# Second-pass products in 64-column tiles, matrix loads in four transfers, and four changed planner settings, in a four-layer graph network on one core

## The chip, the cores and the metric

The kernel runs on one core of a Trainium2 chip. The metric is the device time of one execution in microseconds (us), and lower is better. Before the change it is 1319.26 us, the median of three runs (1314.0 to 1320.12).

## What is computed

There are 32 graphs with 512 nodes and 128 features each (`x`), and one 512 x 512 matrix `adj` of zeros and ones for each graph. Four layers follow one another. Each takes `h = relu(layernorm(x))` and adds its result to `x`:

```python
# 0: masked attention
q, k, v = relu(h @ Wq.T + bq), relu(h @ Wk.T + bk), relu(h @ Wv.T + bv)
x = x + softmax(clip(q @ k.T * adj, 0, 9e13) - 9e15 * (1 - adj)) @ v
# 1: graph convolution, gated by an LSTM that runs over the last 128 nodes' convolved rows
x = x + sigmoid((A_norm @ h) @ lstm(conv(h[:, -128:, :])))
# 2: four sub-layers, each with adj and its transpose, row and column norms, and a tanh
# 3: adj @ (h @ W.T) + bias, with a leaky slope for negative values
```

The LSTM has 128 steps, and each step needs the state `h` of the step before. A step treats all 32 graphs together. It reads only the last 128 nodes of each graph, so attention for those nodes must be finished for every graph before the first step.

## The kernel before

The work is done in three stages. `pass_1` (one call per graph) computes keys, values and the attention of the last 128 nodes, stores keys and values in DRAM, and prepares the LSTM's input. `pass_2` (one call per graph) computes the attention of the other 384 nodes. `rest` does layers 1 to 3 for one graph. The LSTM (`lstm`) runs beside `pass_2`: while one step's cell waits for ScalarE and VectorE, TensorE works on second-pass products.

The second pass of a graph loads keys (`keys`), the normalised input (`hT`), the adjacency matrix (`a`), the values (`v`) and `x`. Line 1303 makes the queries `f_pq`, line 1312 four score blocks `f_s` of 128 x 384, line 1315 their exponentials `f_e`, line 1316 multiplies them by the mask, and line 1321 sums twelve products with the values into `f_po`. Line 1327 adds the result to `xc`, which line 1332 stores in DRAM as `dx`.

All these products are float32. One is issued as two matmul instructions, each with its own weight load. The helper `quarters` (line 1274) cuts a product into four tiles of 32 columns (`TURN`), each a quarter of the output's partitions: eight matmuls and eight weight loads for a product of 128 columns. The LSTM's products `f_z` (line 1223) are also tiles of 32 columns, because their weights are the state of 32 graphs. A step has 16 matmuls: eight with the state of the step before, and eight that prepare a later step's input.

For the graphs in `EARLY` (0 to 23) the second pass goes on. It squares the matrix into `ar` on ScalarE with a row sum (`squares`, line 1360, four operations of one row block each), normalises `xc` in place (lines 1054 and 1057), and makes the first graph sum `f_pg` (line 1406, eight matmuls of 128 x 512 on the whole array), which is stored and read back in `rest`. For the two graphs in `FIRST` (26 and 27) only the squares are made early. For the others the second pass loads 384 columns of the matrix, and `rest` loads it again, whole, in one transfer, and makes the squares and the first sum there. The second pass of the last four graphs (`LATE`) is planned beside `rest`.

The order of the instructions on each engine is fixed when the kernel is built, by a planner (`Plan`). Every operation has a rank, a duration that was written in by hand, and for transfers a `gap`, the time until the data is taken to have landed. The planner lets time run and gives each free engine the lowest-ranked operation that can start. LSTM operations have the lowest ranks. `foresee` notes when the LSTM will next want an engine, and another operation isn't started if it would hold that engine longer than `patience` beyond this time:

```python
elif held is not None and s < held < s + o.engines[e][0] - o.patience:
    continue
```

`patience` is 0.15 us, for the sums of line 1406 `PATIENCE`, 1.3 us. A `SWITCH` time (0.2 us into 128-column products, 0.1 us into tiled ones) is counted where a tiled product meets an untiled one. All tiled products count as one kind. `LANDED` (3.8 us) is the gap of the second pass's loads; other transfers take 2.0. Transfers are issued by SP in the planned order, in one queue.

Operations name the tiles that they read and write, whole (`a`) or by part (`(a, t)`); a whole one conflicts with every part. In the kernel before, line 1291 writes the whole of `a`, and each square reads the whole of it.

Of the kernel before, what the change touches and what calls it, by code (L numbers as in the profile page):

```python
# [13 lines left out]
P = 128  # L14
# [744 lines left out]
def symmetric(ctx, tc, x, adj, weights, cols, rows, lstm_b, prelu_a, out, fail):  # L759
# [12 lines left out]
    nc = tc.nc  # L772
    B, N, D = x.shape
    NT = N // P
    T = P
    L = NT - 1
    NR = N - P
    MANY = 512 // (4 * B)
    LATE = 4
    FIRST = [B - LATE - 2 + k for k in range(2)]  # L780
    EARLY = range(24)
    FOLDS = (4, 7, 10, 13)
    MOVED = range(2, B - 2)
    TURN = 32
    T_STEP = 0.22
    SOON = 9_950.0
    LANDED = 3.8
    PATIENCE = 1.3
    plan_rest = 30_000
    assert D == P and N == 512  # L790

# [14 lines left out]
    def flat(ap):  # L806
        return ap.rearrange("p a b -> p (a b)")

    def f32(ap):
        return ap.bitcast(FP)  # L810
# [5 lines left out]
    def new(tag, shape, name, dtype=FP):  # L816
        return plan.cell(sb, tag, shape, dtype, name)
# [8 lines left out]
    def t_r(n):  # L826
        return max(0.112, n * 0.000455)
# [9 lines left out]
    def t_dma(kb):  # L837
        return 0.1 + kb / 315.0

    def PE(rank, t, fn, r=(), w=(), **k):  # L840
        return plan.op({"PE": (t, fn)}, rank, r, w, **k)

    def ACT(rank, t, fn, r=(), w=(), **k):
        return plan.op({"ACT": (t, fn)}, rank, r, w, **k)
# [7 lines left out]
    def DMA(rank, kb, fn, r=(), w=(), **k):  # L852
        return plan.op({"SP": (max(0.45, t_dma(kb)), fn)}, rank, r, w, gap=k.pop("gap", 2.0), **k)
# [178 lines left out]
    def ln_stats(rank, xc, tiles, name, at=0):  # L1032

        st = new("st", (P, NT, 6), f"f_st_{name}")
        mv = new("mv", (P, NT, 2), f"f_mv_{name}")
        for t in tiles:
            DVE(rank, 0.19, lambda t=t: nc.vector.bn_stats(st.t[:, t, :], xc.t[:, t - at, :]), [(xc, t - at)], [(st, t)])
        for t in tiles:
            DVE(rank, 0.09, lambda t=t: nc.vector.bn_aggr(mv.t[:, t, :], st.t[:, t, :]), [(st, t)], [(mv, t)])
        return mv  # L1040
# [8 lines left out]
    def ln_apply(rank, xc, mean, rstd, shift, r, name, relu=False, place=None):  # L1049

        xn = place or new("xn", (P, NT, P), f"f_xn_{name}")
        for t in range(NT):
            def dve(t=t):
                nc.vector.tensor_scalar(xn.t[:, t, :], xc.t[:, t, :], mean(t), rstd(t), OP.subtract, OP.mult)

            def act(t=t):
                nc.scalar.activation(xn.t[:, t, :], xc.t[:, t, :], AF.Relu, bias=shift(t), scale=rstd(t))
            either = {"ACT": (t_act(P) + 0.13, act)}
            if not relu:
                either["DVE"] = (t_dve(P), dve)  # L1060
            plan.op(either, rank, [(xc, t)] + r, [(xn, t)])
        return xn
# [209 lines left out]


    def quarters(product):
        for k in range(P // TURN):
            product(slice(k * TURN, (k + 1) * TURN))

    def pass_2(b):
        R = 20_000 + b * 10 if b < B - LATE else 30_000 + (b - B + LATE) * 10 + 15
        dkq, dv, dl, dx = kept[b]  # L1280
        early = b in EARLY
        whole = early or b in FIRST
        a = new("a" if whole else "ar", (P, NT, N if whole else NR), f"f_a_{b}")
# [3 lines left out]
        xc = new("x", (P, NT if whole else L, P), f"f_x2_{b}")  # L1287
        DMA(R, 192, lambda: nc.sync.dma_start(hT.t, dkq.t[:, N:]), [dkq], [hT], gap=LANDED)
        DMA(R, 256, lambda: nc.sync.dma_start(keys.t, dkq.t[:, :N]), [dkq], [keys], gap=LANDED)
        if whole:  # L1290
            DMA(R, 1024, lambda: nc.sync.dma_start(a.t, adj[b].rearrange("(t p) j -> p t j", p=P)), [], [a], gap=LANDED)
            ar, deg = squares(R, b, a, "2")
            mask, rows_of = ar, lambda j: f32(ar.t[:, j, :NR])
        else:
            DMA(R, 768, lambda: nc.sync.dma_start(a.t, adj[b, :, :NR].rearrange("(t p) j -> p t j", p=P)), [], [a], gap=LANDED)
            mask, rows_of = a, lambda j: a.t[:, j, :]
        DMA(R, 258, lambda: nc.sync.dma_start(v.t, dv.t), [dv], [v], gap=LANDED)
        DMA(R, 192, lambda: nc.sync.dma_start(xc.t[:, :L, :], x[b, :NR].rearrange("(t p) d -> p t d", p=P)), [],
# [30 lines left out]
        if whole and not early:  # L1329
            begun[b] = a, xc, ar, deg  # L1330
        else:
            DMA(R + 5, 192, lambda: nc.sync.dma_start(dx.t, xc.t[:, :L, :]), [(xc, t) for t in range(L)], [dx])
        mv = ln_stats(R, xc, range(L), f"r{b}")
        l1 = lns[b]
        POOL(R, 0.15, lambda: nc.gpsimd.tensor_copy(ln1[:, b, 0, :L], mv.t[:, :L, 0]), [mv], [(l1, "mr")])
# [19 lines left out]
    def squares(rank, b, a, name):  # L1355

        ar = new("ar", (P, NT, N), f"f_ar{name}_{b}", FR)
        deg = new("dg", (P, NT), f"f_deg{name}_{b}")
        for t in range(NT):
            ACT(rank, 0.62, lambda t=t: nc.scalar.activation(ar.t[:, t, :], a.t[:, t, :], AF.Square,  # L1360
                                                             accum_out=deg.t[:, t : t + 1]), [a], [(ar, t), (deg, t)])
        return ar, deg

    def diagonal(rank, ar, op):
# [5 lines left out]
    def sums_of_1(rank, b, xc, ar, rs):  # L1370
# [4 lines left out]
        xs = ln_apply(rank, xc, lambda t: ln1[:, b, 0, t : t + 1], lambda t: rs.t[:, t : t + 1], lambda t: sh.t[:, t : t + 1],  # L1375
                      [l1, rs, sh], f"c{b}", place=xc if b in EARLY else None)
        xp = relu_parts(rank, xs, f"c{b}")
        pg = bank(f"f_pg_{b}")
        diagonal(rank, ar, OP.add)
        first = aggregate(rank, xp, ar, pg)  # L1380
        gT = xc if b in EARLY else new("gs", (P, N), f"f_gT_{b}")
        evict(rank, N, lambda: gT.t if b not in EARLY else flat(gT.t), lambda: pg.t, [pg], [gT])
        return gT, first
# [10 lines left out]
    def relu_parts(rank, xs, name):  # L1394

        parts = new("y", (P, NT, 2, P), f"f_xp_{name}", FR)
        ACT(rank, 0.52, lambda: nc.scalar.activation(parts.t[:, :, 0, :], xs.t, AF.Relu), [xs], [(parts, 0)])
        DVE(rank, t_dve(N), lambda: nc.vector.scalar_tensor_tensor(  # L1398
            parts.t[:, :, 1, :], xs.t, 0.0, f32(parts.t[:, :, 0, :]), OP.max, OP.subtract), [xs, (parts, 0)], [(parts, 1)])
        return parts  # L1400

    def aggregate(rank, parts, ar, pg):

        def half(k):
            for j in range(NT):
                nc.tensor.matmul(pg.t, parts.t[:, j, k, :], ar.t[:, j, :], start=(k == 0 and j == 0),  # L1406
                                 stop=(k == 1 and j == NT - 1))

        def both():
            half(0)  # L1410
            half(1)
        if rank < plan_rest:
            last = PE(rank, 8 * t_r(N), both, [parts, ar], [pg])
            last.patience = PATIENCE
            return last
        for k in range(2):
            last = PE(rank, 4 * t_r(N), lambda k=k: half(k), [(parts, k), ar], [pg])
        return last

    def rest(b, turn, lw_after):  # L1420
# [12 lines left out]
        l1 = lns[b]  # L1433
        rs = None if b in EARLY else new("rs", (P, NT), f"f_rs_c{b}")

# [12 lines left out]

        if b in EARLY:
            gT, first = new("gs", (P, N), f"f_gT3_{b}"), None  # L1450
# [157 lines left out]
    for b in range(B):  # L1608
        pass_2(b)
        if b in FOLDS:  # L1610
            fold(FOLDS.index(b), 20_000 + b * 10)
# [89 lines left out]
```

## Time and profile before

| | before |
|---|---|
| median of the runs shown | 1319.26 us |
| the profiled execution, its own time | 1317.18 us |
| span of its instructions | 1315.4 us |
| TensorE, weight loads (busy in the span) | 1275.1 us (97%), 974.1 us (74%) |
| VectorE, ScalarE, GpSimd | 992.6 (75%), 833.2 (63%), 392.4 (30%) |
| `f_z` line 1223, 2040 matmuls | 87.0 us |
| `f_s` line 1312, 1024 matmuls | 106.6 us |
| `f_po` line 1321, 3072 matmuls | 108.6 us |
| `f_pq` line 1303, 256 matmuls | 27.7 us |
| instruction fetches | 97 packets, 1.59 MB |
| mean granted clock of TensorE | 0.994 |

Busy time is the time in which at least one instruction of the group has a record open. A record of a matmul lasts longer than its data streams, since its end is modelled, so the pace of the array is read from the distance between the starts of records. A line of the timeline has the start, the time to the end of the merged records, the engine, the line of the code, the operation, what it writes and reads, the shape and the count; in brackets stands idle time before it and what ended it. "issue" means that the engine waited for nothing that the profile shows. A line of waits has the waiting engine and line, what it waited for, the total in us, the number of times and the longest. A line by stretch has the start and end of the stretch, its length, busy time and instruction count of TensorE, its weight loads, VectorE, ScalarE and GpSimd, then TensorE's granted clock, the share of the DMA engines and their GB/s.

### The profile page before, as it was taken

Reading aid. Unit: us, or ns where it says so; the run is one execution under the profiler, and the core shown is the slowest. Engines: PE = TensorE matmul, PEld = TensorE weight load, DVE = VectorE, ACT = ScalarE, POOL = GpSimd, SP = SyncE. Lnnn points to the kernel's source line nnn. Section 1 sums busy time; section 2 is a strip of 40 time slices with the busy share of each in tenths; the row PEclk is TensorE's granted clock in tenths of the full one; section 3 lists DMA queues with packets and bytes.
Section 4 is the critical chain, followed back from the end, with each engine's and each line's share of the span. In section 5 each row is a group of like instructions: output and inputs, shape, how many; then the busy total and the mean of one; then the engine's idle time right before and its main releaser. Section 6 shows DMA issues by size and latency. Waiting matters only on the chain.

```text
span 1315.4 us, 32850 instructions
## 1 busy us (share of the span) xinstructions
PE 1275.1 (97%) x12097; PEld 974.1 (74%) x12098; DVE 992.6 (75%) x3286; ACT 833.2 (63%) x2095; POOL 392.4 (30%) x737
## 2 busy tenths in 40 slices
PE   8999999999899899999999999999999999999997
PEld 6888866666576666777777878778787787787774
DVE  7998877767788786977676767777676777787654
ACT  5666757667587565577566666666666675676423
POOL 4655532212242222443031322313222132242101
PEclk9999999999999899999999999999999999999999
DMA  8888888766777555999576677777777755673311
GB/s 264 257 277 279 274 272 254 250 214 205 225 243 243 151 165 163 216 213 207 130 158 159 155 156 163 164 158 152 154 164 161 165 120 90 151 170 72 49 33 35
DMA packets 300585, 234.50 MB, mean 178 GB/s; under 512 B 138240, under 2 KB 244480, under 8 KB 300416
## 3 DMA queue, kind: packets, MB, share of 16 engines
q1 hardware_dynamic: 283520, 215.54, 59.4%
q0 software_dynamic: 16896, 16.78, 8.1%
q8 instruction: 97, 1.59, 0.5%
q14 instruction: 72, 0.59, 0.1%
HBM read 138.16 MB, written 62.65 MB: 153 GB/s over the span
## 4 chain that ended last, share of the span: by engine, by line
PE 84%; DVE 6%; DMA 4%; ACT 3%; issue 2%; POOL 1%; SPq 0%; ACTq 0%; DVEq 0%; POOLq 0%
PE f_pa L1406 17%; PE f_py L1510 15%; PE f_pa L1521 14%; PE f_pg L1406 9%; PE f_s L1312 4%; PE f_z L1223 4%; PE f_po L1321 4%; PE f_p L1562 2%; PE f_pol L1173 2%; PE f_pk L1130 2%; PE f_pv L1146 2%; PE f_pl L1464 2%; PE f_sl L1163 2%; DMA f_a<-in_adj_dram 2%; PE f_pd L1198 1%
## 5 line engine op out<-in xcount | busy, mean ns | idle before, releaser
L1406 PE MATMUL f_pa<-f_ar,f_y 128*128 128x512 f32 x1024 | 300.5, 430 | 1.6 <-ACT f_y L1389 1.4
L1406 PEld LDWEIGHTS f_pa<-f_ar,f_y 128*128 128x128 f32 x1024 | 189.4, 188 | 77.9 <-issue 39.9
L1510 PE MATMUL f_py<-f_wf,f_n 128*128 128x128 f32 x1280 | 173.8, 275 | 0.0
L1510 PEld LDWEIGHTS f_py<-f_wf,f_n 128*128 128x128 f32 x1280 | 165.0, 191 | 9.6 <-issue 2.4
L1521 PE MATMUL f_pa<-f_n,f_wf 128*128 128x512 f32 x320 | 153.1, 592 | 0.0
L1525 ACT ACTIVATE f_n<-f_pa,f_bcol 128x512 f32<-128x512 f32 x128 | 88.2, 689 | 92.1 <-PE f_pa L1521 92.1
L1360 ACT ACTIVATE f_ar<-f_a 128x512 fp32r<-128x512 f32 x224 | 138.7, 622 | 6.0 <-DMA f_a<-in_adj_dram 4.6
L1389 ACT CAST f_y<-f_py 128x512 fp32r<-128x512 f32 x128 | 74.8, 585 | 102.3 <-PE f_py L1510 95.3
L1478 POOL DMA_DIRECT2D f_das<-f_ar x32 | 27.0, 842 | 370.5 <-ACT f_ar L1360 309.3
L1312 PE MATMUL f_s<-f_q,f_k 128*32 128x384 f32 x1024 | 106.6, 500 | 6.4 <-issue 5.7
L1321 PE MATMUL f_po<-f_v,f_e 128*32 128x129 f32 x3072 | 108.6, 273 | 4.3 <-issue 4.2
L1321 PEld LDWEIGHTS f_po<-f_v,f_e 128*32 128x32 f32 x3072 | 90.7, 110 | 22.8 <-issue 14.2
L1517 DVE TENSOR_TENSOR f_pa<-f_pa,f_inv 128x512 f32<-128x512 f32 x128 | 86.7, 693 | 26.3 <-PE f_pa L1406 25.8
L1390 DVE TENSOR_TENSOR f_y<-f_py,f_y 128x512 fp32r<-128x512 f32 x128 | 87.4, 684 | 22.2 <-ACT f_y L1389 22.2
L1223 PE MATMUL f_z<-f_w,f_seq 128*32 128x128 f32 x2040 | 87.0, 280 | 13.0 <-DVE f_seq L1268 5.9
L1223 PEld LDWEIGHTS f_z<-f_w,f_seq 128*32 128x32 f32 x2040 | 55.1, 110 | 51.0 <-ACT f_e L1315 12.2
L1521 PEld LDWEIGHTS f_pa<-f_n,f_wf 128*128 128x128 f32 x320 | 57.5, 190 | 44.8 <-issue 36.8
L1483 DVE SCALAR_TENSOR_TENSOR f_junk<-f_a,f_aT 128x1024 bf16<-128x1024 f32 x64 | 78.1, 1221 | 3.0 <-DMA f_aT<-f_das 1.1
L1315 ACT ACTIVATE f_e<-f_s 128x384 f32<-128x384 f32 x128 | 61.5, 484 | 26.0 <-PE f_s L1312 14.1
L1406 PE MATMUL f_pg<-f_ar,f_xp_d 128*128 128x512 f32 x256 | 74.2, 413 | 0.3 <-DVE f_xp_d L1398 0.2
L1085 DVE COPY f_hl_d<-f_n 128x1024 uint16<-128x1024 uint16 x28 | 19.4, 693 | 70.9 <-ACT f_n L1525 70.8
L1510 PE MATMUL f_py<-f_wf,f_T_c 128*128 128x128 f32 x448 | 72.8, 275 | 0.0
(203 smaller groups left out, 2763.8 us busy)
## 6 DMA issues: line engine op xcount, KB each, us to landing
f_a<-in_adj_dram SPq DMA_DIRECT2D x56, 1024.0 KB
f_das<-f_ar POOLq DMA_DIRECT2D x32, 512.0 KB, 4.7
f_dkq<-f_kh SPq DMA_DIRECT2D x32, 448.0 KB
f_dv<-f_v SPq DMA_DIRECT2D x32, 258.0 KB
f_v<-f_dv SPq DMA_DIRECT2D x32, 258.0 KB
f_x<-in_x_dram SPq DMA_DIRECT2D x32, 256.0 KB
f_al<-in_adj_dram SPq DMA_DIRECT2D x32, 256.0 KB
f_k<-f_dkq SPq DMA_DIRECT2D x32, 256.0 KB
```

What stands on the lines that cost most here:

```text
L1223: nc.tensor.matmul(z.t[part, k, :, :], h, w[:, m : m + 4, part], start=False, stop=True, skip_group_check=True)
L1312: PE(R, t_mm(NR), lambda s=s, j=j: quarters(lambda p: nc.tensor.matmul(s.t[p], keys.t[:, j * P + p.start : j * P + p.stop], q.t, start=Tru ...
L1321: PE(R, t_mm(P), lambda t=t, j=j: quarters(lambda p: nc.tensor.matmul(po.t[p, t, :], es[j].t[:, t * P + p.start : t * P + p.stop], v.t[:, ...
L1360: ACT(rank, 0.62, lambda t=t: nc.scalar.activation(ar.t[:, t, :], a.t[:, t, :], AF.Square, accum_out=deg.t[:, t : t + 1]), [a], [(ar, t), ...
L1389: ACT(rank, t_act(N), lambda: nc.scalar.copy(parts.t[:, :, 0, :], src.t), [src], [(parts, 0)])
L1390: DVE(rank, t_dve(N), lambda: nc.vector.tensor_sub(parts.t[:, :, 1, :], src.t, f32(parts.t[:, :, 0, :])), [src, (parts, 0)], [(parts, 1)])
L1406: nc.tensor.matmul(pg.t, parts.t[:, j, k, :], ar.t[:, j, :], start=(k == 0 and j == 0), stop=(k == 1 and j == NT - 1))
L1483: nc.vector.scalar_tensor_tensor(junk, flat(a.t[:, 2 * k : 2 * k + 2, :]), 1.0, flat(aT.t[:, 2 * k : 2 * k + 2, :]), OP.mult, OP.not_equal ...
L1510: nc.tensor.matmul(py.t[:, j, :], nodes[n].t[:, bass.ts(j, P)], wf[:, W_F[i] + c, 0, :], start=False, stop=(c == nch - 1), skip_group_chec ...
L1517: before = DVE(R, t_dve(N), lambda pa=pa: nc.vector.tensor_mul(pa.t, pa.t, inv_row.t), [inv_row], [pa])
L1521: nc.tensor.matmul(pa.t, wf[:, W_F[i] + c, 1, :], nodes[n].t, start=False, stop=(c == nch - 1), skip_group_check=True)
L1525: ACT(R, 0.57, lambda pa=pa, n=n, i=i: nc.scalar.activation(n.t, pa.t, AF.Tanh, bias=bcol[:, i : i + 1]), [pa], [n])
```

## The change

`quarters` now makes two tiles of 64 columns instead of four of 32. It is used for the products of lines 1303, 1312 and 1321. The LSTM's tiles stay at 32 columns, and the planner's durations and its one kind of tiled product stay as they are.

The second pass loads the matrix in four transfers, one for each row block, and a square depends on its own row block. In `rest` the load stays one transfer.

Four settings change: `EARLY` is 0 to 21 (graphs 22 and 23 join those whose squares and first sum are made in `rest`), `PATIENCE` is 0.9 us, and a new `STORED`, 5.0 us, is the gap of the store of `xc` on line 1332, in place of the ordinary 2.0 us. The planner works out a new order from all of this.

```diff
-    EARLY = range(24)
+    EARLY = range(22)
 ...
-    PATIENCE = 1.3
+    STORED = 5.0
+    PATIENCE = 0.9
 ...
     def quarters(product):
-        for k in range(P // TURN):
-            product(slice(k * TURN, (k + 1) * TURN))
+        for k in range(0, P, 2 * TURN):
+            product(slice(k, k + 2 * TURN))
 ...
         if whole:
-            DMA(R, 1024, lambda: nc.sync.dma_start(a.t, adj[b].rearrange("(t p) j -> p t j", p=P)), [], [a], gap=LANDED)
+            for t in range(NT):
+                DMA(R, 256, lambda t=t: nc.sync.dma_start(a.t[:, t, :], adj[b, t * P : (t + 1) * P, :]), [], [(a, t)], gap=LANDED)
 ...
         else:
-            DMA(R, 768, lambda: nc.sync.dma_start(a.t, adj[b, :, :NR].rearrange("(t p) j -> p t j", p=P)), [], [a], gap=LANDED)
+            for t in range(NT):
+                DMA(R, 192, lambda t=t: nc.sync.dma_start(a.t[:, t, :], adj[b, t * P : (t + 1) * P, :NR]), [], [(a, t)], gap=LANDED)
 ...
-            DMA(R + 5, 192, lambda: nc.sync.dma_start(dx.t, xc.t[:, :L, :]), [(xc, t) for t in range(L)], [dx])
+            DMA(R + 5, 192, lambda: nc.sync.dma_start(dx.t, xc.t[:, :L, :]), [(xc, t) for t in range(L)], [dx], gap=STORED)
 ...
             ACT(rank, 0.62, lambda t=t: nc.scalar.activation(ar.t[:, t, :], a.t[:, t, :], AF.Square,
-                                                             accum_out=deg.t[:, t : t + 1]), [a], [(ar, t), (deg, t)])
+                                                             accum_out=deg.t[:, t : t + 1]), [(a, t)], [(ar, t), (deg, t)])
```

## The prediction

> **What bounds the kernel now.** I read the page first (TensorE busy 97% of the span, and 84% of the chain that ended last), then busy time by stretch, because the change touches one stage only. The stretch from 184 to 522 us holds the LSTM's products `f_z`; 545 to 1250 is the third stage.
>
> ```profile
> 184.00:522.00 338.00, 313.82 (x6188) 214.42 (x6188) 263.87 (x1083) 229.87 (x814) 87.30 (x163) 0.98 0.67 211
> 545.00:1250.00 705.00, 703.46 (x3809) 550.16 (x3808) 518.51 (x1355) 459.38 (x990) 197.43 (x308) 1.00 0.68 150
> ```
>
> The first pair of numbers after the length is TensorE. In the third stage it is never free, and the change leaves most of its products as they are. In the LSTM stretch 24 us are free, and more is lost that counts as busy, because a matmul's record lasts longer than the array streams. So I took start-to-start times of matmul records: 338 us for 128 steps, 2.64 us a step on average, but 2.38 at the median. The 16 steps that lose over 0.9 us against their matmuls' streaming lose 31 us together. What a step is made of, TensorE alone in order of time:
>
> ```profile
> 399.73 0.65 PE L1223 MATMUL f_z<-f_w,f_seq 128*32 128x128 f32 x16
> 400.19 2.17 PE L1321 MATMUL f_po<-f_v,f_e 128*32 128x129 f32 x72
> 402.18 0.62 PE L1223 MATMUL f_z<-f_w,f_seq 128*32 128x128 f32 x16
> 402.62 0.62 PE L1321 MATMUL f_po<-f_v,f_e 128*32 128x129 f32 x16
> ...
> 404.57 0.62 PE L1223 MATMUL f_z<-f_w,f_seq 128*32 128x128 f32 x16
> 405.12 2.11 PE L1406 MATMUL f_pg<-f_ar,f_xp_c 128*128 128x512 f32 x8
> 407.15 0.65 PE L1223 MATMUL f_z<-f_w,f_seq 128*32 128x128 f32 x16
> ```
>
> From `f_z` to `f_po`, both 32 columns wide, 16 records take 0.44 to 0.46 us. From `f_z` to the 128-column `f_pg` they take 0.55. Nine `f_po` products, of four tiles and two records each, take 1.99 us, 0.221 each. A 128-column float32 product of line 1510 takes two records 0.112 apart, 0.224. Column width gives no throughput here; one width for LSTM and filler saves switches.
>
> The long steps have two causes. One is a hole inside a product, with no semaphore in it:
>
> ```profile
> 425.72 0.48 PE L1312 MATMUL f_s<-f_q,f_k 128*32 128x384 f32 x1
> 429.71 0.86 PE L1312 MATMUL f_s<-f_q,f_k 128*32 128x384 f32 x4 [3.51 <-issue]
> ```
>
> Such holes stand at 218.9, 328.7, 392.5 and 425.7 us and cost 2.33, 3.23, 1.86 and 3.67 beyond streaming, 11.1 together. Each ends 1.3 to 1.4 us after a packet of the instruction queue ended, and that packet started 5.5 to 7.4 us after a 1 MB matrix load (line 1291) was issued. The other cause stands in the waits of the stretch:
>
> ```profile
> DVE f_x L1054 <- DMA f_dx<-f_x: 7.1, 5, 2.1
> ACT f_x L1057 <- DMA f_dx<-f_x: 5.8, 3, 2.1
> ```
>
> VectorE and ScalarE stand, with the LSTM's cell operations queued behind them, until the store of `xc` has been read, since the in-place normalisation overwrites it. The plan believed in 2.0 us.
>
> **What the Trainium skill says.** "TensorEngine Tiling (Array Packing)", Tiling Modes, Key Properties: changing the tiling mode drains the engine, changing the tile does not. The trace agrees for 32 against 128 columns, and says nothing of 32 against 64. "Runtime: NRT & Kernel Launch", Instruction fetch mechanics: instructions come in 16 KiB blocks of 256 by a DMA queue of the sequencer's own. The page's 97 instruction packets with 1.59 MB are such blocks, and 24,195 matmuls and weight loads would need 95. "DMA: Bandwidth & Descriptors", Queues, rings and completion order: a DMA engine serves its rings in turn and changes only at a packet's end. The trace shows the delay behind a 1 MB load, not the rule. "TensorE: Matmul & The Clock Gate", Part 1: an idle window of about 3.4 us brings the clock to half. The records show half clock for 3.4 us at 333 and 6.8 us at 429, after the two longest holes.
>
> **The change part by part**, against the profiled execution's 1317.2 us (span 1315.4, 1.8 around it).
>
> *64-column tiles.* 4352 records on lines 1303, 1312 and 1321 become 2176, and as many weight loads go: 4352 instructions, 17 of 97 fetches. Streaming stays at 0.22 a product by the two widths on either side, so 0 us. What is added is a switch wherever LSTM and filler meet. By the order of the records there are 127 intervals between steps; 108 begin and 85 end with a second-pass product (the others with a 128-column one, where a switch is paid already). Price: into 128 columns, the first weight load starts 0.201 us after the last `f_z` record, which streams 0.107: an empty array for 0.094. Then the first record lasts 0.499 against 0.391, so its weights take 0.106 more. Back to 32 columns, `f_pg` to `f_z` is 0.319 start to start against 0.213 of streaming, 0.106, and 0.297 against 0.273 shows 0.024 for the weights. Between 0.024 and 0.106, 64 columns would have some 0.051 (an estimate). So 0.145 into 64 and 0.128 into 32, if this pair drains. Sum: 108 x 0.145 + 85 x 0.128 = 26.5 us. Bounds: 0, if the pair does not drain; 108 x 0.200 + 85 x 0.130 = 32.7 at 128-column prices. The cover is TensorE waiting for h before `f_z`: 18.3 us in all, 39 steps with over 0.1. Interval by interval it leaves 17.3 of the 26.5. Some of that cover sits in the stalled steps and goes with them, and a filler product that is 0.145 late also makes the exponential late that stands ahead of the LSTM's tanh on ScalarE. I take +22.
>
> *Matrix loads in four.* The wait of a fetch behind one load shrinks to about a quarter if the ring is left between loads, and the fetches are fewer. At stake: 11.1 of holes and some 3.1 for the half clock (steps of 3.74, 3.41 and 3.17 us against 2.4). The squares can start at the first quarter, but ScalarE waited only 4.6 us for matrices in the whole span, so that is worth nothing. It adds 3 x 32 = 96 issues to SP's queue, 0.3 to 0.45 us each, about 1.3 us a batch, ahead of v and x of the same batch; SP has room (the timeline shows gaps of 4 us), and the plan prices the four at 3.65 for 3.35. A load that came late would hold ScalarE at the square and the tanh behind it. Bounds -14 and +3; I take -10, since other loads stay in front of fetches and a new order makes collisions of its own.
>
> *STORED.* The store is now given 5.0 us. The waits of 7.1 and 5.8 overlap in time; four of the long steps are theirs (241, 310, 357 and 454 us, 1.9 + 1.4 + 1.9 + 2.0 lost, some 0.3 each of it ordinary): 6 at stake, bounds -6 and 0, taken -5.
>
> *EARLY 22 and PATIENCE 0.9.* Two `f_pg` groups, 2 x 8 x 0.231 = 3.7 us of TensorE, leave the LSTM stretch for the third stage; second-pass products that now end at 545 move up into their place. Eight squares go, and 2 x 256 KB each of stores, loads and the matrices' last columns. PATIENCE forbids the latest starts of `f_pg`: four steps of about 3.48 us, at most 0.4 each. Bounds -3 and +4, taken 0. In the third stage two batches get a diagonal, a split and a sum of their own, the two sums being those 3.7 us.
>
> Sum: +22 - 10 - 5 + 0 = +7 to 8, so about 1325 for an execution like the profiled one. The median is 2.1 above that one: **1327 us**, 0.6% slower. A measurement of this kernel tells about 0.5%, 6.6 us, from no change.
>
> **Rivals.**
> - *It balances.* The holes and the store waits go whole and the waits for h hide switches down to 17: 17 - 14 - 6 = -3, 1316 us (1311 to 1321). For it: the holes' timing behind matrix loads is regular. Against it: each new order of some 30,000 instructions has stalls of its own.
> - *No drain between 64 and 32 columns* (the other side). Both widths use all rows and differ only in column groups; if the array takes the new weights without emptying, the switches cost 0 and -14 - 6 remain: 1299 us (1294 to 1308). Against it: the 32-to-128 switch, which empties the array here, and the page, which speaks of modes and not of rows. The point: with 15 us of gain and 97 pairs of switches of which some 83% are uncovered, it is faster by over 0.5% when a pair costs under (15 - 6.6) / 80 = 0.10 us; I expect 0.27.
> - *The gains do not come.* If the ring holds all four loads ahead of the fetch as before, or ScalarE now waits for quarters, the switches stand alone: +26, 1345 us (1337 to 1350).
>
> **How the numbers follow.** Forecast 0.43 (its own range 1321 to 1336), balance 0.23, no drain 0.17, no gains 0.12, anything else 0.05. Slower by over 0.5% (above 1326): two thirds of the forecast, all of "no gains", a little else, 0.43. Faster (below 1312.7): no drain and a third of the balance, 0.27. Within: 0.30. The range 1299 to 1344 cuts half of "no drain" and half of "no gains" off.
>
> **What would show it.** Between `f_z` and a second-pass product the 16 records should take about 0.55 instead of 0.45 us, and the first record after a switch should be longer than the rest; equal times mean no drain. Second-pass groups at half the count and unchanged start-to-start time show the streaming right. Instruction packets near 80 and no holes marked issue over 1 us show the fetch right. `f_dx` should be gone from the waits. The LSTM stretch should last about 345 us instead of 338. If the third stage, not this stretch, carries the difference, the EARLY step is wrong.

## The result and the profile after

The changed kernel takes 1313.6 us, the median of 20 runs (1311.46 to 1315.27). The kernel before, run beside it, takes 1316.51 us (20 runs, 1312.19 to 1324.0). The ratio is 0.9969, 95% interval 0.9954 to 0.9984: faster by 0.3%, and less than the 0.5% that the prediction set as a bound for a difference. The forecast was 1327 us. The profiled execution took 1312.57 us, with a span of 1310.7 us against 1315.4 before: 4.7 us shorter.

Three stretches of the changed kernel, with the columns of the prediction's first view:

```profile
184.00:522.00 338.00, 333.52 (x4382) 214.23 (x4383) 270.89 (x1123) 233.23 (x814) 92.14 (x170) 0.99 0.70 219
522.00:545.00 23.00, 20.86 (x143) 16.34 (x142) 15.38 (x43) 14.54 (x38) 9.86 (x15) 0.93 0.79 214
545.00:1250.00 705.00, 702.83 (x3815) 551.24 (x3814) 516.12 (x1336) 455.84 (x978) 193.71 (x295) 1.00 0.65 144
```

In the first line TensorE's busy time has grown by 20 us, and its instructions have fallen from 6188 matmuls to 4382. The busy column misleads here: the LSTM doesn't end at 522 any more but at 502, and what follows is other work. So I count from the first `f_z` to the last, and how long the array streams in between (the number of records of each kind by its undisturbed start-to-start time):

| | before | after |
|---|---|---|
| first to last `f_z` | 337.1 us | 317.8 us |
| of it streaming, and not streaming | 271.8, 65.3 | 261.8, 56.0 |
| last `f_z` to the end | 793.9 us | 808.5 us |
| of it streaming, and not streaming | 741.8, 52.1 | 751.8, 56.7 |
| steps that lose over 0.9 us, and their loss | 16, 31.0 us | 2, 4.0 us |
| median step | 2.38 us | 2.49 us |

The LSTM's part is 19.3 us shorter, but 10.0 of that is work that moved behind it (four groups of `f_pg`, some 7 us, and some 3 of second-pass products). The array stands idle 9.3 us less in the LSTM's part and 4.6 us more behind it: 4.7 together, the change of the span.

The two long steps that are left follow one another. In the first TensorE waits for the state, in a step without other work:

```profile
351.43 0.64 PE L1224 MATMUL f_z<-f_w,f_seq 128*32 128x128 f32 x16 [1.83 <-DVE f_seq L1269]
```

The second runs its eight `f_pg` matmuls at half clock (3.4 us from 352.1), and from the first of them to the next `f_z` it takes 3.61 us, against 2.03 in the step at 405 us before. So half clock didn't go with the holes: it also came after this wait of 1.83 us, and after one of 1.44 behind the LSTM, both shorter than the 3.4 us that the prediction took over for an idle window.

The tiled products on the page before and after, first before, with the instruction fetches:

```profile
q8 instruction: 97, 1.59, 0.5%
...
L1321 PE MATMUL f_po<-f_v,f_e 128*32 128x129 f32 x3072 | 108.6, 273 | 4.3 <-issue 4.2
L1321 PEld LDWEIGHTS f_po<-f_v,f_e 128*32 128x32 f32 x3072 | 90.7, 110 | 22.8 <-issue 14.2
```

```profile
q8 instruction: 81, 1.33, 0.4%
...
L1324 PE MATMUL f_po<-f_v,f_e 128*64 128x129 f32 x1536 | 103.3, 277 | 0.0
L1324 PEld LDWEIGHTS f_po<-f_v,f_e 128*64 128x64 f32 x1536 | 86.0, 136 | 23.2 <-issue 16.5
```

Half the count, the same time for one record, 16 fetches fewer, and the 4.3 us of idle time ended by "issue" have gone to 0.0. So have the waits for `f_dx`. In the waits of the stretch from 184 to 545 us the changed kernel has two for a transfer, one of 0.5 us and this:

```profile
DVE f_junk L1486 <- DMA f_aT<-f_das: 1.1, 1, 1.1
```

TensorE in order of time, changed kernel:

```profile
398.45 0.64 PE L1224 MATMUL f_z<-f_w,f_seq 128*32 128x128 f32 x16
399.02 2.21 PE L1324 MATMUL f_po<-f_v,f_e 128*64 128x129 f32 x36
401.17 0.64 PE L1224 MATMUL f_z<-f_w,f_seq 128*32 128x128 f32 x16
401.74 2.11 PE L1409 MATMUL f_pg<-f_ar,f_xp_c 128*128 128x512 f32 x8
```

From `f_z` to `f_po` is now 0.57 us, as long as to the 128-column `f_pg`; it was 0.46. Record by record, at the median, the last `f_z` to the first `f_po` takes 0.203 (before some 0.07), the first record after a switch lasts 0.324 against 0.273, and back to `f_z` it is 0.202 (before 0.090). Each switch has the price that the prediction worked out. Nine products still take 36 records and 0.222 us each.

### The profile page after: what moved, and what is told of

Its sections match the earlier page's. It is cut to its first block, busy times and chain, and to the rows that moved or that the text cites. A ratio compares the mean times of both kernels' runs of the same rounds, so it can differ in the third digit from the quotient of the medians.

```text
span 1310.7 us, 28591 instructions
## 1 busy us (share of the span) xinstructions
PE 1287.5 (98%) x9921; PEld 967.2 (74%) x9921; DVE 990.5 (76%) x3274; ACT 837.4 (64%) x2093; POOL 394.2 (30%) x733
## 4 chain that ended last, share of the span: by engine, by line
PE 91%; DVE 3%; POOL 2%; DMA 1%; ACT 1%; issue 1%; SPq 0%; ACTq 0%; POOLq 0%; DVEq 0%
PE f_pa L1409 17%; PE f_py L1513 15%; PE f_pa L1524 15%; PE f_pg L1409 9%; PE f_po L1324 7%; PE f_s L1315 6%; PE f_z L1224 5%; PE f_p L1565 2%; PE f_pol L1174 2%; PE f_pl L1467 2%; PE f_pv L1147 2%; PE f_pk L1131 2%; PE f_sl L1164 2%; PE f_pq L1306 2%; PE f_pd L1199 1%; PE f_xt_a L859 1%
## 5 line engine op out<-in xcount | busy, mean ns | idle before, releaser
L1409 PE MATMUL f_pa<-f_ar,f_y 128*128 128x512 f32 x1024 | 294.9, 425 | 0.5 <-ACT f_y L1392 0.5
L1363 ACT ACTIVATE f_ar<-f_a 128x512 fp32r<-128x512 f32 x216 | 133.7, 622 | 5.0 <-PE f_pg L1409 3.2
L1324 PE MATMUL f_po<-f_v,f_e 128*64 128x129 f32 x1536 | 103.3, 277 | 0.0
L1324 PEld LDWEIGHTS f_po<-f_v,f_e 128*64 128x64 f32 x1536 | 86.0, 136 | 23.2 <-issue 16.5
L1315 PE MATMUL f_s<-f_q,f_k 128*64 128x384 f32 x512 | 99.8, 496 | 0.0
L1224 PE MATMUL f_z<-f_w,f_seq 128*32 128x128 f32 x2040 | 82.5, 278 | 4.7 <-DVE f_seq L1269 2.5
L1224 PEld LDWEIGHTS f_z<-f_w,f_seq 128*32 128x32 f32 x2040 | 48.3, 109 | 48.4 <-issue 10.8
L1318 ACT ACTIVATE f_e<-f_s 128x384 f32<-128x384 f32 x128 | 61.5, 488 | 17.0 <-PE f_s L1315 11.9
L1058 ACT ACTIVATE f_xn_c<-f_x,f_sh_c,f_rs_c 128x128 f32<-128x128 f32 x138 | 58.0, 486 | 21.8 <-DVE f_sh_c L1066 21.7
```

What stands on the lines that cost most here:

```text
L1224: nc.tensor.matmul(z.t[part, k, :, :], h, w[:, m : m + 4, part], start=False, stop=True, skip_group_check=True)
L1315: PE(R, t_mm(NR), lambda s=s, j=j: quarters(lambda p: nc.tensor.matmul(s.t[p], keys.t[:, j * P + p.start : j * P + p.stop], q.t, start=Tru ...
L1324: PE(R, t_mm(P), lambda t=t, j=j: quarters(lambda p: nc.tensor.matmul(po.t[p, t, :], es[j].t[:, t * P + p.start : t * P + p.stop], v.t[:, ...
```

## The experiments

Ratios are to the kernel before, run beside it on the same chip, with 95% intervals. "Holes" are stops of TensorE in which its last instruction stands at three quarters of a block of 256, and which end 1.2 to 1.6 us after an instruction packet. All of TensorE's instructions count here, its waits for semaphores beside the matmuls and weight loads, from the program's start: in the trace before the last one is number 192 of its block every time. That trace has seven, 14.0 us between starts (the prediction knew four of them). Stops under some 0.55 us between starts aren't counted; they would add up to 1.5 us to a kernel's sum.

### The width of the tiles, with the order held

The planner doesn't see the width. A kernel that differs only in it has the same order on all engines, so a pair can be read step against step.

`x1_cols32`: the changed kernel with 32-column tiles.

```diff
-        for k in range(0, P, 2 * TURN):
-            product(slice(k, k + 2 * TURN))
+        for k in range(P // TURN):
+            product(slice(k * TURN, (k + 1) * TURN))
```

> The changed kernel with the second pass back in four tiles of 32 columns; everything else of the change stays. Theory: the switches between LSTM and filler cost the changed kernel some 20 us, and the quarter loads alone have removed the instruction holes: about 1294 us (1288 to 1300), median step of the LSTM stretch near 2.3 us, holes inside a product under 3 us in all. Rival, the narrower instruction stream of the 64-column tiles removed the holes: they come back here (10 to 14 us with the half clock), 1303 to 1308. Rival, the switches cost nothing to the end because the time is given back after the LSTM: 1310 to 1316.

Measured: 1313.17 us, ratio 0.9973 (0.9954 to 0.9991), the same as the changed kernel. Two steps of it, and then the same two of the changed kernel, on TensorE:

```profile
268.14 0.65 PE L1224 MATMUL f_z<-f_w,f_seq 128*32 128x128 f32 x16 [0.23 <-DVE f_seq L1269]
268.58 1.50 PE L1315 MATMUL f_s<-f_q,f_k 128*32 128x384 f32 x16
270.30 0.64 PE L1224 MATMUL f_z<-f_w,f_seq 128*32 128x128 f32 x16 [0.22 <-DVE f_seq L1269]
...
398.69 0.64 PE L1224 MATMUL f_z<-f_w,f_seq 128*32 128x128 f32 x16
399.15 2.17 PE L1324 MATMUL f_po<-f_v,f_e 128*32 128x129 f32 x72
401.14 0.63 PE L1224 MATMUL f_z<-f_w,f_seq 128*32 128x128 f32 x16
```

```profile
268.96 0.65 PE L1224 MATMUL f_z<-f_w,f_seq 128*32 128x128 f32 x16
269.53 1.51 PE L1315 MATMUL f_s<-f_q,f_k 128*64 128x384 f32 x8
271.12 0.65 PE L1224 MATMUL f_z<-f_w,f_seq 128*32 128x128 f32 x16
```

The first step takes 2.16 us in both: TensorE waited 0.22 for the state `h`, and the switches take the place of that wait. The second (the changed kernel's is in the fence further up, 398.45 to 401.17) takes 2.72 against 2.45: full of work, it pays the whole pair of switches, 0.27. Steps of the two kernels can be matched by the work in them, and I call one calm that loses no more than 1.6 us in either, beside what its own products other than `f_z` stream. The 117 calm ones are longer by 12.0 us together; the seven others are shorter by 7.7. The 32-column kernel has 8.5 us of holes, the changed one none. From the first `f_z` to the last the changed kernel takes 2.8 us more (317.8 against 315.0), and behind it 4.3 us less: there it waits 1.44 us instead of 3.01 for the first transposes, and half clock follows for 3.4 us instead of 6.8.

`x2_before_cols64`: the kernel before with 64-column tiles.

```diff
-        for k in range(P // TURN):
-            product(slice(k * TURN, (k + 1) * TURN))
+        for k in range(0, P, 2 * TURN):
+            product(slice(k, k + 2 * TURN))
```

> The kernel before with the second pass in two tiles of 64 columns and nothing else; the planner's order is the one of before. Theory: switches +20, the holes mostly stay because the fetch still waits for a 1 MB load, though a block of instructions now lasts longer: -5, so about 1331 us (1325 to 1338). Rival, fewer instructions alone cure the holes: -14, 1322 and no hole over 1 us. Rival, no cost of switches: 1302 to 1312.

Measured: 1314.57 us, ratio 0.9976 (0.9958 to 0.9993). 107 calm steps are 13.9 us longer, the holes go from 14.0 us to none. No load and no setting was touched: the wider tile alone takes the holes away. What it doesn't take away are the store waits. In this trace one wait for `f_dx` of 5.4 us made one step 5.0 us late.

`x7_quarters_cols64`: the kernel before with four-transfer loads and 64 columns, and the old settings. Its 32-column counterpart is `x4_before_quarters` below.

```diff
+            for t in range(NT):
+                DMA(R, 256, lambda t=t: nc.sync.dma_start(a.t[:, t, :], adj[b, t * P : (t + 1) * P, :]), [], [(a, t)], gap=LANDED)
...
+        for k in range(0, P, 2 * TURN):
+            product(slice(k, k + 2 * TURN))
...
```

> The kernel before with loads in four transfers and 64-column tiles, and the three settings as before. Both parts alone were 0.4 and 0.2% faster than before, and if both remove the same instruction holes they don't add: 1309 to 1314, no hole at the end of a fetched block. If the parts were independent: 1308 or less. If the settings carry the change: 1314 or more.

Measured: 1318.28 us, ratio 1.0005 (0.9987 to 1.0024), against 0.9963 with 32 columns. Calm steps pay 11.5 us, and there were only 8.1 us of holes to save.

`x5_after_cols128`: the changed kernel with whole products.

```diff
-        for k in range(0, P, 2 * TURN):
-            product(slice(k, k + 2 * TURN))
+        product(slice(0, P))
```

> The changed kernel with the second-pass products whole, 128 columns wide, in the same order of instructions: only the width of the switch changes. If a switch costs an empty array of 0.094 us and then the weights of the first product, going out to 128 columns costs 0.055 us more than to 64 at some 105 places, less what waits hide: +3 to +6, so 1316 to 1320, no instruction holes, step median near 2.54 us. If switches are hidden, 1312 to 1315.

Measured: 1312.06 us, ratio 0.9963 (0.9948 to 0.9978); 72 fetches, no holes. A step of second-pass products alone is 0.052 longer than with 64 columns, and the other calm steps are 0.047 shorter, since `f_pg` and second-pass products no longer differ.

`x8_after_split`: the changed kernel with each 64-column matmul cut in two along the moving columns. This keeps the 64-column tiles and has, again, the instruction count of 32 columns (`f_pq` and `f_po` are cut in the same way).

```diff
-            PE(R, t_mm(NR), lambda s=s, j=j: quarters(lambda p: nc.tensor.matmul(
-                s.t[p], keys.t[:, j * P + p.start : j * P + p.stop], q.t, start=True, stop=True)), [keys, q], [s], tiled=True)
+            PE(R, t_mm(NR), lambda s=s, j=j: quarters(lambda p: [nc.tensor.matmul(
+                s.t[p, c : c + NR // 2], keys.t[:, j * P + p.start : j * P + p.stop], q.t[:, c : c + NR // 2], start=True, stop=True) for c in (0, NR // 2)]), [keys, q], [s], tiled=True)
```

> The changed kernel with each second-pass product of 64 columns issued in two halves of its moving columns (192 of 384, 65 and 64 of 129), so that the number of instructions is that of 32-column tiles again and the switches stay. If the number of instructions makes the holes: 98 packets, 4 to 9 holes of 8 to 14 us with half clocks behind the longest, 1321 to 1329. If column width itself removed them: none, and 1313 to 1316, unless the halves of 65 columns stream slower, which the start-to-start times would show.

Measured: 1327.07 us, ratio 1.0083 (1.0051 to 1.0115), by the ratios 1.1% or 15 us above the changed kernel, with 98 fetches. Only 2.5 us of that are holes, in two places, where 8 to 14 us were expected if the number of instructions makes them. A product takes 0.234 instead of 0.222 us, and the calm steps grow by 8.7 us. So this run shows the price of twice the instructions on one width, but for the holes it speaks only in part: two came back, and most did not. The part on the prediction has what the packets show.

### The loads

`x4_before_quarters`: the kernel before with loads in four and squares by part.

```diff
-            DMA(R, 1024, lambda: nc.sync.dma_start(a.t, adj[b].rearrange("(t p) j -> p t j", p=P)), [], [a], gap=LANDED)
+            for t in range(NT):
+                DMA(R, 256, lambda t=t: nc.sync.dma_start(a.t[:, t, :], adj[b, t * P : (t + 1) * P, :]), [], [(a, t)], gap=LANDED)
...
```

> The kernel before with matrix loads of the second pass in four transfers and squares by row block, and the new order that follows. Theory: the fetch of instructions gets in between loads, the four holes (11 us) and the half clock (3 us) go: about 1305 us (1301 to 1310), instruction packets 97 and no hole over 1 us. Rival, the ring holds all four loads ahead of the fetch: holes of 8 us or more stay and the time is 1313 to 1320.

Measured: 1310.99 us, ratio 0.9963 (0.9944 to 0.9981), holes 8.1 us instead of 14.0. But the order is another one, in which the waits for `f_dx` fell from 12.9 to 3.0 us too.

`z1_before_split_same_order`: one planned operation issues all four, so the order stays.

```diff
-            DMA(R, 1024, lambda: nc.sync.dma_start(a.t, adj[b].rearrange("(t p) j -> p t j", p=P)), [], [a], gap=LANDED)
+            DMA(R, 1024, lambda: [nc.sync.dma_start(a.t[:, t, :], adj[b, t * P : (t + 1) * P, :]) for t in range(NT)], [], [a], gap=LANDED)
...
```

> The kernel before with each 1 MB matrix load issued as four transfers by one planned operation, so that the planner's order of all engines stays as it was and the squares still wait for all four. If an instruction fetch gets in between the four, the holes inside products shrink from 14.0 us to under 5 and the time falls to 1303 to 1309. If the queue's ring holds all four ahead of the fetch, the holes stay near 14 us and the time is 1314 to 1318; then what the four-transfer kernels gained came from their new order and not from the transfers' size.

Measured: 1312.2 us, ratio 0.9959 (0.9937 to 0.998), and neither forecast fits. First before, then `z1`, at the two places that were the longest holes before:

```profile
328.15 0.83 PE L1321 MATMUL f_po<-f_v,f_e 128*32 128x129 f32 x18
332.05 1.31 PE L1321 MATMUL f_po<-f_v,f_e 128*32 128x129 f32 x38 [3.07 <-issue]
```

```profile
328.02 0.83 PE L1321 MATMUL f_po<-f_v,f_e 128*32 128x129 f32 x19
331.38 2.37 PE L1321 MATMUL f_po<-f_v,f_e 128*32 128x129 f32 x37 [2.52 <-issue]
...
424.58 0.48 PE L1312 MATMUL f_s<-f_q,f_k 128*32 128x384 f32 x1
427.36 0.53 PE L1312 MATMUL f_s<-f_q,f_k 128*32 128x384 f32 x4 [2.29 <-issue]
```

3.07 became 2.52, and 3.51 (in the prediction's view) became 2.29; in all 12.3 us of holes against 14.0. That would fit a fetch which still waits behind most of the four; no run shows it directly. The profiled execution was the slowest of its twelve runs, though (1317.58 us), so its holes may be above the usual.

`w1_split_same_order_cols64` and `w2_split_same_order_cols128`: `z1` with 64-column tiles (the diff) and with whole products, as in `x5`.

```diff
-        for k in range(P // TURN):
-            product(slice(k * TURN, (k + 1) * TURN))
+        for k in range(0, P, 2 * TURN):
+            product(slice(k, k + 2 * TURN))
```

> The kernel before with the matrix loads split by one planned operation and 64-column tiles: the planner's order of before in all, with both direct parts of the change and none of its settings. In this order 64 columns alone gave a ratio of 0.9976 and the split alone 0.9959. If the split acts only through the waits for instructions, which 64 columns have taken away already, the two don't add: 0.997 to 0.999, 1313 to 1316. If it acts through something else, such as other transfers that come sooner, they add: 0.992 to 0.995, 1306 to 1310.

> The same with second-pass products of 128 columns, so that the tile's width is the only difference to the 64-column and the 32-column kernel with split loads in this order. If waits for instructions are what wider tiles save and a switch to 128 costs 0.055 us more than one to 64, some 100 times, up to 5 us above the 64-column one; if the waits for h take that up, equal, within 2 us.

Measured: `w1` 1313.35 us, ratio 0.9995 (0.9978 to 1.0013); `w2` 1309.12 us, ratio 0.9945 (0.9925 to 0.9965). In one and the same order 64 columns alone gave -0.2%, the split alone -0.4%, and both about nothing. The gains don't add. This fits the view that both work on the waits for instructions, and `w1`, by its ratio just above what was expected for that, leaves little room for another gain of the split. That 128 columns are 4.2 us faster than 64 was not expected. In the two traces the span differs by 2.0 us, and the first `f_z` already comes 2.2 us sooner; the cause is open. `w2` is the fastest kernel of the study, but its interval overlaps the changed kernel's, which was run on another chip.

### The settings

`x3_before_stored`: the kernel before with the store's gap at 5.0 us.

```diff
+    STORED = 5.0
...
-            DMA(R + 5, 192, lambda: nc.sync.dma_start(dx.t, xc.t[:, :L, :]), [(xc, t) for t in range(L)], [dx])
+            DMA(R + 5, 192, lambda: nc.sync.dma_start(dx.t, xc.t[:, :L, :]), [(xc, t) for t in range(L)], [dx], gap=STORED)
```

> The kernel before with a gap of 5.0 us for the store of xc, and the new order that follows. Theory: waits for that store leave the list of VectorE and ScalarE in the LSTM stretch, and 5 us go: about 1311 us (1306 to 1315). Rival, the time is lost elsewhere because the in-place normalisation and the sum after it start later: 1316 or more.

Measured: 1329.55 us, ratio 1.0094 (1.0057 to 1.0131). The waits for `f_dx` fell from 12.9 us to 0.9, and the kernel got slower by 12 us: in the new order there are ten holes, 15.0 us, waits for matrices of 4.7, and 9.2 us more of idle array behind the LSTM (61.3 against 52.1).

`x6_after_stored2`: the changed kernel with 2.0 us.

```diff
-    STORED = 5.0
+    STORED = 2.0
```

> The changed kernel with the store of xc at a gap of 2.0 us again, with the order that follows. If the gap was worth the store waits: those waits come back (VectorE and ScalarE on f_dx, 5 us or more) and the time is 1316 to 1321. If the setting only shuffled the order: 1309 to 1315.

Measured: 1324.47 us, ratio 1.0046 (1.003 to 1.0063), by the ratios 0.8% or 10 us above the changed kernel, with 6.0 us of waits for `f_dx` back. One setting is 12 us of loss in one order and 10 of gain in the other.

`y4_before_settings` and `z2_settings_cols64`: the kernel before with the three settings, and the same with 64 columns.

```diff
-    EARLY = range(24)
+    EARLY = range(22)
-    PATIENCE = 1.3
+    STORED = 5.0
+    PATIENCE = 0.9
...
```

> The kernel before with the settings alone (EARLY 22, PATIENCE 0.9, STORED 5.0), loads in one transfer, 32 columns. If the settings are good in themselves: 1305 to 1314. If they only fit the order that the four loads give, as the store's gap alone did (13 us slower): 1318 to 1330.

> The kernel before with the three settings (22 early batches, patience 0.9, stores counted as 5.0 us) and 64-column tiles, but whole matrix loads. With the settings alone it was 1328 and with 12 holes of 18.1 us. If the order that the settings make carries that loss, 1326 (1322 to 1330) though no hole is left; if the holes were the loss, 1318 or less, since 64 columns take them all away.

Measured: `y4` 1328.14 us, ratio 1.008 (1.0054 to 1.0105), twelve holes of 18.1 us; `z2` 1320.22 us, ratio 1.0023 (1.0001 to 1.0045), between the two forecasts. Taking 18.1 us of holes away saved 7.5 us (0.57%) and not the whole loss; calm steps pay 10.8. The rest stays in the order.

`y5_after_early24` and `y6_after_patience13`: the changed kernel with one old setting each.

```diff
-    EARLY = range(22)
+    EARLY = range(24)          # y5 alone
...
-    PATIENCE = 0.9
+    PATIENCE = 1.3             # y6 alone
```

> The changed kernel with all 24 early batches again. If a setting acts only through the order that it happens to give, anywhere in 1309 to 1326. If the second chunk of work left for the third stage is a cost of its own, 1309 to 1311, since 3.7 us of products move back into the LSTM stretch.

> The changed kernel with patience 1.3 again. If a setting acts only through the order that it happens to give, anywhere in 1309 to 1326. If late starts of 128-column groups delayed steps as the prediction had it, 1314 to 1316 and four steps of the LSTM near 3.5 us.

Measured: 1316.29 us, ratio 0.9984 (0.9968 to 1.0001), and 1315.1 us, ratio 0.9986 (0.997 to 1.0001). Each is some 2 us worse, inside the intervals. With 24 early graphs the LSTM's part still has 160 records of `f_pg`, as with 22: the planner finds no time for more, so this setting moved nothing there.

All eight combinations, ratio to before:

| | 32 columns | 64 columns |
|---|---|---|
| whole loads, old settings | 1 | 0.9976 |
| whole loads, new settings | 1.0080 | 1.0023 |
| four loads, old settings | 0.9963 | 1.0005 |
| four loads, new settings | 0.9973 | 0.9969 |

The same settings cost 0.8% with whole loads and 32 columns and gain 0.36% with four loads and 64 columns. Each of the three parts gains beside some values of the other two and loses, or gives nothing, beside others.

### What the planner is told, and the passage to the next layers

`y3_after_switch_known`: the planner counts 32 and 64 columns as two kinds and charges 0.13 and 0.15 us between them.

```diff
-    SWITCH = (0.2, 0.1)
+    SWITCH = (0.2, 0.13, 0.15)
...
-                    [es[j], v], [po], tiled=True)
+                    [es[j], v], [po], tiled=2)
```

> The changed kernel with a planner that counts a switch between 32 and 64 columns too (0.15 us into 64, 0.13 into 32). If the unplanned switches put the engines out of step with the plan, a plan that knows them wins some of their 15 us back: 1300 to 1310. If they are a plain cost on TensorE: 1311 to 1318, the spread being that of a new order.

Measured: 1330.63 us, ratio 1.0105 (1.0066 to 1.0144). The LSTM takes 304.4 us, the shortest of all, but only 238.2 us of streaming were put beside it (261.8 in the changed kernel). The part behind it takes 842.1 us. A short LSTM isn't a short kernel.

`y1_after_no_compare` and `y2_cols32_no_compare`: the changed kernel and `x1_cols32` without VectorE's comparison of the matrix with its transpose for the first two graphs of `rest`; this part of the computation is left out.

```diff
+                if turn < 2:
+                    nc.vector.memset(viol[:, b, k : k + 1], 0.0)
+                    return
```

> The changed kernel in the same order of instructions, but for the first two graphs of the third stage VectorE's comparison of the matrix with its transpose is left out (a fill of the result's cells stands in its place, so these two graphs are not checked for symmetry). Theory: at the passage from the LSTM to the third stage TensorE waits for a normalisation that stands behind these comparisons; without them the hole before the transposes near 529 us (1.4) and the half clock after it (3.4 us at half) go: 1309 to 1312. Rival, the passage is bound by something else: 1313 to 1315 with the hole still there.

> The same (two graphs' comparison left out) in the kernel with the whole change but 32-column tiles. There the hole at the passage was 3.0 us and the half clock 6.8 us long: theory 1306 to 1309 against 1313.2; rival 1312 to 1315.

The reason is the stretch behind the LSTM in the changed kernel, where its idle time grew. VectorE, GpSimd, ScalarE and TensorE:

```profile
526.67 1.20 DVE L1486 SCALAR_TENSOR_TENSOR f_junk<-f_a,f_aT 128x1024 bf16<-128x1024 f32 x1
...
530.07 0.16 DVE L1066 SCALAR_TENSOR_TENSOR f_sh_c<-f_mv_c,f_rs_c 128x4 f32<-128x4 f32 x1 [0.92 <-POOL f_rs_c L1047]
530.26 1.65 ACT L1058 ACTIVATE f_xn_c<-f_x,f_sh_c,f_rs_c 128x128 f32<-128x128 f32 x4 [6.01 <-DVE f_sh_c L1066]
530.81 1.48 PE L859 MATMUL f_xt_c<-f_ident,f_xn_c 128*128 128x128 f32 x4 [1.44 <-ACT f_xn_c L1058]
```

The comparison stands on VectorE while the normalisation waits, and TensorE then waits for it. Without it: 1313.96 us, ratio 0.9978 (0.9962 to 0.9995), and 1312.16 us, ratio 0.9964 (0.9946 to 0.9982), nothing gained. The next transfer waited for in that place, `y1` and then `y2`, is ScalarE's for the whole matrix that `rest` loads:

```profile
ACT f_ar L1363 <- DMA f_a<-in_adj_dram: 2.8, 1, 2.8
```

```profile
ACT f_ar L1363 <- DMA f_a<-in_adj_dram: 5.8, 1, 5.8
```

TensorE's longest idle time there moved by some microseconds and grew, from 1.44 to 2.17 us and from 3.01 to 5.24. So the passage has at least two limits that end within a few microseconds of one another, and the comparison alone isn't what it costs.

## Why the prediction was wrong

The forecast was +7 to 8 us; measured were -2.9 by the medians and -4.7 by the spans. 2.7 us of the miss lie in the starting point, since the median of three runs, 1319.26, was above that of twenty. Step by step:

**The switch price was right, its sum was not.** "If this pair drains": it does. The Trainium skill, "TensorEngine Tiling (Array Packing)", Key Properties, keeps the drain to a change of the tiling mode; here 32 to 64 columns over all 128 rows behaves as such a change, and a pair costs 0.27. The rival "no drain" is refuted. But in five pairs with the order held (`x1` and the changed kernel, before and `x2`, `x4` and `x7`, `y4` and `z2`, `z1` and `w1`), 107 to 120 calm steps out of some 126 grew by 12.0, 13.9, 11.5, 10.8 and 12.5 us, or 12 to 16 for all steps at the same rate (10 to 14 in the calm ones, wherever between 1.1 and 1.6 us the limit for calm is put). The step "I take +22" failed: it started from the covered sum, 17.3, and added to it for secondary delays that the runs don't show. A wait for `h` of 0.22 hides nearly the whole pair, as in the step at 268 us; that such waits hid more than was counted follows from the sums, and wasn't counted step by step.

**The holes: right in kind, credited to the wrong part, and too small.** All of them went, 14.0 us, against 11.1 listed. But the step "matrix loads in four, -10" had them as the loads' doing and named the lower count of fetches in half a sentence. By `x2`, wider tiles remove all of them in the old order; by `z1`, the split alone leaves 12.3 us in its trace. The working that was missing: a run of `f_po` uses up a block of 256 instructions, sixteen products of sixteen instructions at 0.222, in 3.55 us with 32 columns and in 7.1 with 64.

The traces show what that does, when blocks are counted from where the holes stand. Before, in the LSTM's part, a block's packet ended 0.3 to 7.2 us after the block ahead of it was begun (median 3.5), and a block lasted 4.1 to 11.9 us (median 6.5); 17 of 49 blocks began less than 1.8 us after their packet, the earliest 1.1. In the changed kernel packets ended as late, 0.4 to 7.8 us (median 2.7), but a block lasted at least 6.6 us (median 9.2), and each of the 33 packets had ended 2.5 us or more before its block began. The longer block covers the late fetch. `x8` has blocks about as short as `x1` (median 6.5 and 6.0 us), but only 3 of its 49 packets ended over 4.5 us after the block ahead was begun, against 9 in `x1` and 14 in the kernel before. So its few holes go with sooner packets; why they came sooner is open.

That blocks of 256 are fetched, as "Runtime: NRT & Kernel Launch", Instruction fetch mechanics, says, agrees with the place of every hole. That crossing into one is mostly hidden holds here by count and not by cost: of 49 crossings with 32 columns seven weren't hidden, and took 14.0 us.

**STORED, -5: its own wait was right, as an edit it has no value of its own.** The waits for `f_dx` are gone, and with them the four long steps, some 6 us by the prediction's own reading of them. But by the same edit the kernel before lost 12 us (`x3`), and by taking it back the changed kernel lost 10 (`x6`). The prediction priced an edit of the plan by the wait that it removes, and left out that a new order is drawn.

**EARLY and PATIENCE, 0: right in size,** within 2 us (`y5`, `y6`), though not in the working: not two but four `f_pg` groups moved, and `y5` shows that the setting didn't move them.

**Not priced: +4.6 us behind the LSTM.** "If the third stage, not this stretch, carries the difference, the EARLY step is wrong" was too simple a test. Both parts changed by far more than the result, -19.3 and +14.6 us, because 10 us of work moved. Part of the 4.6 us is the wait of 1.44 us for the transposes and the half clock after it (3.4 us from 533.0), which the trace before doesn't have; the rest is open.

The terms as measured: 13 for the switches, -14 for the holes, -6 for the store waits, +4.6 behind the LSTM, together -2.4 against the 4.7 us by which the span fell. The likeliest rival, "It balances" (+17 - 14 - 6, 1316 us), was nearest, in sum and in mechanism. Its gain of 20 is the size found, though its 14 was made up of 11 us of holes and 3 of half clock; its switches were 4 too dear, and it too had nothing for the passage. What isn't settled is why the order alone moves this kernel by 12 us either way. In `x3` and `y4` there are more holes than before (15.0 and 18.1 us) and 9 and 12 us more idle time behind the LSTM. `x6` has no holes; against the changed kernel its array stands idle 10 us longer in the LSTM's part and 5 behind it. No run separates these.

## What to carry to other kernels

Where a planned order stands as close to the limit of its bounding engine as here, an edit that makes the planner draw again may be first of all a new draw: in this kernel one was worth up to 12 us either way. Hold the order still to price an edit, and price the settings together with what they were chosen for. Count an engine's idle time over the whole run, not the length of one stage, as work moves across the stage's end. And when a stop stands inside a run of small matmuls, ask how fast that run uses up instructions, and not only which transfer was in the way.

## What the runs showed that was not expected

Run-to-run scatter goes with the holes, in the main. The standard deviation is 3.5 to 5.0 us for the kernel before (20 to 59 runs at a time), 2.6 to 3.0 for the 32-column kernels with split loads (`x4`, `x1`, `y2`, `z1`), and 1.2 to 2.3 for all kernels with 64 or 128 columns but one (1.2 for the changed kernel, `x5` and `x7`; 3.0 for the six runs of `y3`). This would fit executions that differ in how many fetches come late, but with one trace a kernel it isn't shown.

A float32 product of 129 moving columns takes 0.222 us in four tiles of 32 columns, two of 64 or one of 128 (0.223). In this case the width costs only at the switch: weights of 64 columns lengthen the first record by 0.051, which the prediction had interpolated between 0.024 and 0.106. In the page of the fastest kernel, `w2`, one weight load has become longer and the product hasn't:

```profile
q8 instruction: 72, 1.18, 0.4%
...
L1320 PEld LDWEIGHTS f_po<-f_v,f_e 128*128 128x128 f32 x768 | 97.1, 191 | 21.8 <-issue 9.1
L1320 PE MATMUL f_po<-f_v,f_e 128*128 128x129 f32 x768 | 107.4, 281 | 0.0
```
